# Half-width products of a graph attention issued in a fixed order, with one third of them moved behind the next tile

## The chip, the cores and the metric

The kernel runs on one core of a Trainium2 chip. The metric is the device time of one execution in microseconds (us): 3205.59 is the median of three runs before the change. The core's engines are TensorE (PE; its weight loads are PEld), VectorE (DVE), ScalarE (ACT), GpSimd (POOL) and SyncE (SP); each works through its own instructions in an order fixed when the kernel is built, and waits for the others through semaphores. All data are 32-bit floats.

## The reference, cut to what matters

Two graph layers over 4096 nodes with 512 features in 4 heads of 128. The first layer has an encoder attention, an MLP, a decoder attention and another MLP; the second layer is an attention of another kind. The change is in the decoder attention, which multiplies the encoder's attention matrix once more with new values:

```python
sig = jax.nn.sigmoid(f1[:, :, None] + f2[:, None, :])
...
att = ALPHA * long_att + (1.0 - ALPHA) * local_att
...
Yh = emb.reshape(n, H, D).transpose(1, 0, 2)
Y = jnp.einsum('hij,hjd->hid', att, Yh)
Y = jnp.einsum('hnd,hed->hne', Y, W)
Yc = Y.transpose(1, 0, 2).reshape(n, F)
Yc = jax.nn.elu(Yc)
out = _mlp_block(Yc, dec_mlp_W, dec_mlp_b, dec_mlp_bn_gamma, dec_mlp_bn_beta)
```

The unnormalised weight of node i for node j is exp(sigmoid) where the adjacency is 1, and 0 elsewhere. The kernel gets the sigmoid from a Tanh, and the sums that normalise are kept from the encoder.

## The kernel before

**Blocks and tiles.** The decoder attention is one call of `attention` (L836). It has 8 blocks: 4 heads times 2 halves of the target nodes (2048 columns, `TB`). A block goes through 32 weight tiles, j = 0 to 31, each of 128 source nodes by 2048 targets. Of every five tiles the last (j = 4, 9, 14, 19, 24, 29) is read back from memory, where the encoder had put it (L421, on SyncE's queue); the other 26 are made: Tanh on ScalarE (L568), Exp on ScalarE in place (L569), multiplied by the mask on VectorE in place (L570). The mask `a` comes by SyncE (L212).

**Buffers of tiles.** `weight_tile` takes two of every seven tiles from one pool with two buffers and five from another with five. The Tanh of a later tile can start when a buffer of its pool has been read for the last time.

**Products.** TensorE accumulates a block's output (128 features by 2048 targets) in four banks `po`. Every product of the decoder has a stationary operand of 64 columns and writes the lower (g = 0) or upper (g = 1) 64 partitions of a bank, so it uses one side of the array; two products on different sides can run at once. A single tile takes 8 products: 4 banks times 2 sides.

**Pairs.** To save products, 8 pairs of tiles, (5,6), (8,9), ... (26,27), are handled by sums in the manner of Strassen's scheme: 14 products in place of 16. For a pair with tiles e1 and e2, each with a left and a right half of 1024 columns, VectorE makes t0 = e1 left + e1 right (L331), t1 = t0 + e2 right (L335), t2 = t1 + e2 left (L340), and e1's right half becomes e1 right + e2 right: in block 0 on VectorE (L339), in blocks 1 to 7 by an accumulating DMA on POOL's queue (L337). The tiles t0, t1, t2 have two buffers each. The stationary operands z0 to z3 of the pairs (L816 to L822) lie in the tile `w`, which later holds the next MLP's weights. The products of a pair, in `seven` (L342), go to three sums:

- `po[2]`, `po[3]` with z3 and e2 right (2 products), and `po[0]`, `po[1]` with e2 left and t2 (4);
- `aux[0]`, `aux[1]` with e1 left and t1 (4);
- `aux[2]`, `aux[3]` with t0 and the summed e1 right (4): this is called the third sum below.

So `po` and `aux` take all 8 banks, and the two sets change places from block to block. After the last pair, at j = 31, ScalarE copies `aux` out (L369), POOL's queue swaps its halves (L373), and in the next block at j = 2 VectorE adds it all up (`combined`, L383 to L388). At j = 3 VectorE adds `po` (L806, L809); scaling and ELU follow (L684, L830 to L832).

**What sets the order.** The program is written to a library that places each engine's instructions itself, from its own estimate of when operands will be ready and from the order in which they were made. A dependency given by hand, `tc.issue_after(x)`, keeps instructions of the same engine behind x. In the decoder no such dependency ties the products to each other: `halves` (L326) only makes a product. In blocks 1 to 7 of the trace the products are in the order in which they were made; in block 0 they are not.

**At the end.** `decoder_weights` (L824) loads the next MLP's weights into `w` on SyncE's queue. It is made in the last block at j = 28, and waits for the last product that reads z.

Of the kernel before, what the change touches and what calls it, by code (L numbers as in the profile page):

```python
# [39 lines left out]
N, F, H, D, P = 4096, 512, 4, 128, 128  # L40
# [5 lines left out]
TB = 2048  # L46
NTB = N // TB
# [30 lines left out]
HB = TB // 2  # L78
HD = D // 2
# [10 lines left out]
def kernel(ctx, tc, x, xT, adjT, w0, w0T, v0, wencT, wdecT, vecs, w1, w1T, a1, outT):  # L90
    nc = tc.nc
# [131 lines left out]
    def attention(what, keep, pools, weights, values, row_of, out, finish, ebufs, modes=None, invert=None,  # L223
# [25 lines left out]
        spool, made, masks0 = pools, 0, list(masks0)  # L249
# [73 lines left out]
        pairs = [FIRST + STEP * k for k in range(PAIRS)] if fast is not None else []  # L323
        banks8 = [*(bank() for _ in range(7)), bank1()] if fast is not None else []

        def halves(b, g, weight, x, start, stop):  # L326
            return nc.tensor.matmul(b[g * HD:(g + 1) * HD, :], weight, x, start=start, stop=stop)  # L327

        def sums_first(e):
            t = [spool.tile([P, HB], FP, name=f"t{k}", tag=f"t{k}", bufs=2) for k in range(3)]  # L330
# [11 lines left out]
        def seven(k, v, po, aux, t, e1, e2):  # L342

            one = block(v, pairs[k])
            two = block(v, pairs[k] + 1)
            z = [fast[0][:, i, k, :] for i in range(4)]
            first, stop = k == 0, k == PAIRS - 1

            def into(b, g, weight, x, part, aux_bank):
                return halves(b, g, weight, x[:, part * IB:(part + 1) * IB], first and aux_bank, stop and aux_bank)  # L350

            into(po[2], 0, z[3], e2[:, HB:TB], 0, False)
            into(po[3], 1, z[3], e2[:, HB:TB], 1, False)
            for part in range(2):
                into(aux[part], 0, one[:, 0:HD], e1[:, 0:HB], part, True)
                into(aux[part], 1, z[1], t[1], part, True)
            for part in range(2):
                into(po[part], 0, two[:, 0:HD], e2[:, 0:HB], part, False)
                into(po[part], 1, two[:, HD:D], t[2], part, False)
            for part in range(2):  # L360
                into(aux[2 + part], 0, z[0], t[0], part, True)
                made = into(aux[2 + part], 1, z[2], e1[:, HB:TB], part, True)
            return made

        def aux_out(h, tb, aux, m):
# [27 lines left out]
        for n, (h, tb) in enumerate(blocks):  # L393
# [14 lines left out]
            for j in range(NJ):  # L408

                with pinned(products_of):  # L410
                    for f in later.pop(j, []):
                        f()
                with pinned([a_load, *products_of, last_main] if j else []):
                    if (n, j) in extras:
                        extras[n, j](a_load)
                    if not last and j == NJ - 10:
                        next_row = next_row_of(*blocks[n + 1])
                e = weight_tile()
                store = j % KEEP == KEEP - 1 and kept is not None
                if store and kept == "read":  # L420
                    a_load = nc.sync.dma_start(e, ekeep[h][tb][j // KEEP])  # L421
                else:
                    if masks0:
                        a, a_load = masks0.pop(0)
                    else:
                        a = mask_tile(keep)
                        a_load = load_mask(a, tb, j)

                    with pinned([*(products_of[:1] if kept == "read" and n == 0 and j < 8 else ()),
                                 *(behind if n == 0 and j < EP else ())]):  # L430
                        products_of = weights(e, rowb, a, j, h, SB if NJ * n + j < in_parts0 else 1)


                    if stores and (store if n > 1 else j % KEEP == KEEP - 3):
                        k, t = stores.pop()
                        (nc.sync if n > 1 else nc.scalar).dma_start(ekeep[h][tb][k], t)
                    if store:
                        stores.append((j // KEEP, e))

                if j in pairs:  # L440
                    e1, sums_of = e, sums_first(e)
                elif j - 1 in pairs:
                    made_sums = sums_second(sums_of, e1, e, n > 0)
                    products_of = products_of[0], made_sums

                def products():
                    nonlocal last_main, last_ones
                    if fast is not None:
                        if j - 1 in pairs:
                            last_main = seven(pairs.index(j - 1), values[h], po, aux, sums_of, e1, e)  # L450
                        elif j not in pairs:
                            for s, b in enumerate(po):
                                for g in range(2):
                                    f = (g + s // (SB - 1)) % 2
                                    last_main = halves(b, g, block(values[h], j)[:, f * HD:(f + 1) * HD],
                                                       e[:, s * IB:(s + 1) * IB], j == 0, j == NJ - 1)
                        return

                    with tc.issue_after(last_ones.ins) if last_ones is not None else nullcontext():

                        if j == EVICT:
                            po.append(bank())
                            for k, t in ahead:
                                nc.tensor.matmul(po[-1], block(values[h], k), t[:, (SB - 1) * IB:SB * IB],
                                                 start=(k == 0), stop=False)
                        for s, b in enumerate(po):
                            last_main = nc.tensor.matmul(b, block(values[h], j), e[:, s * IB:(s + 1) * IB],  # L467
                                                         start=(j == 0), stop=(j == NJ - 1))
                    last_ones = None


                if last and invert is not None and j >= NJ - (1 if kept is not None else 4):
                    late.append((j, e))
                else:
                    products()
                if j < EVICT and fast is None:
                    ahead.append((j, e))
                if fast is not None and j == pairs[-1] + 1:
                    m = []
                    at(NJ - 1, aux_out, h, tb, aux, m)  # L480
                    if not last:
                        at(2, combined, h, tb, m)
                if invert is not None:
                    if j in moved:

                        for into_half, e_half in in_parts(2, into, e):
                            nc.gpsimd.dma_start(into_half, e_half, **({"accum_op": ALU.add} if j > moved[0] else {}))  # L487
                    elif j in by_ones:
                        held.append(e)
                    else:  # L490
                        adds.append(e)
                        if last and kept is not None and j >= NJ - 6:
                            at_end.append(e)
                        elif len(adds) == 2:
                            nc.vector.tensor_add(acc, *adds)
                        elif len(adds) > 2:
                            nc.vector.tensor_add(acc, acc, e)  # L497

                    if j == NJ - 1:
                        for t in at_end:  # L500
                            nc.vector.tensor_add(acc, acc, t)

                    if held and j + 1 not in by_ones:
                        with tc.issue_after(last_main.ins):
                            for t in held:
                                add_to_den(den, t, not begun)
                                begun = True
                        held = []
                    if j == NJ - 1:
                        with tc.issue_after(last_ones.ins) if last_ones is not None else nullcontext():  # L510
                            if moved and not ends_later:
                                add_to_den(den, into, not begun)
                                begun = True
                            add_to_den(den, acc, not begun, not ends_later)
# [60 lines left out]
    with tc.tile_pool(name="keep", bufs=1) as keep:  # L575
# [259 lines left out]
        with tc.tile_pool(name="dec", bufs=1) as spool:  # L835
            attention("dec", keep, spool, tanh_weights, xc, lambda h, tb: (rows[tb], h), out_dec, (scaled, elu), 5,  # L836
                      kept="read", behind=behind_it, fast=(z, xd, stationaries),
                      extras={(H * NTB - 1, 28): decoder_weights})


    v1 = xd
# [283 lines left out]
```

## Time and profile before

| what | us |
|---|---|
| median of the runs (3205.39 to 3206.06) | 3205.59 |
| the profiled execution: its own time | 3206.21 |
| the profiled execution: its span on the core | 3204.4 |
| decoder attention, from its first product to its last, at 1182.8 and 2028.6 | 845.8 |
| granted TensorE clock over the execution | 0.996 |

Times in the profile count from the start of the span. A row of a timeline gives the start, the duration, the engine, the line, the operation, output <- inputs, the shape and the number of instructions that were merged; in brackets stands how long the engine had been idle, and what ended that. A product of 32-bit floats leaves two records, each written down as 0.59 us long; records that follow one another on one side of the array start 0.43 us apart, and those of the two sides overlap. The name `ps` stands for seven of the banks, and `den` for the eighth; `e,R` is a weight tile with a value block, `t` a sum, `w` the stationary operands z.

### The profile page before, as it was taken

To read this page: it belongs to the slowest core of one execution; us is meant where nothing else is said; L and a number is where in the kernel's file an instruction comes from. 1 tells how busy PE (TensorE), PEld (TensorE's weight loads), DVE (VectorE), ACT (ScalarE), POOL (GpSimd) and SP (SyncE) were. 2 spreads that over 40 slices of the span, in tenths; PEclk is the share of its full clock that TensorE was granted. 3 is DMA by queue.
4 is the path that set the end of the run, shared out by engine and by line. 5 is a ranking of instruction groups with operands and counts; after the bars stand their busy time and mean duration, and the time that the engine had idled before them with its cause. 6 is when DMAs were issued, how large, how long until landed. Compare 5 with 4: busy or idle time off the path is not lost.

```text
span 3204.4 us, 30115 instructions
## 1 busy us (share of the span) xinstructions
PE 3146.2 (98%) x10467; PEld 1375.5 (43%) x10467; DVE 2944.2 (92%) x2229; ACT 2570.7 (80%) x1825; POOL 567.8 (18%) x740
## 2 busy tenths in 40 slices
PE   7999999999999999999999999999999999999998
PEld 6334444444444464333333333458544444444443
DVE  7989999999999679999999999785699999999998
ACT  7999999999998449999999999456755665666663
POOL 3001211211211000111111111026312222222211
PEclk9999999999999999999999999999999999999999
DMA  9998988988987013667776676331579999999986
GB/s 211 198 193 252 270 223 229 269 221 231 271 230 193 7 43 128 193 188 205 211 200 181 202 217 183 104 112 60 157 188 234 215 221 243 219 214 229 234 213 157
DMA packets 223433, 620.71 MB, mean 194 GB/s; under 512 B 26832, under 2 KB 29936, under 8 KB 207280
## 3 DMA queue, kind: packets, MB, share of 16 engines
q0 software_dynamic: 79648, 263.41, 43.2%
q1 hardware_dynamic: 132200, 332.53, 30.3%
q10 hardware_dynamic: 11432, 22.85, 2.0%
q8 instruction: 82, 1.34, 0.2%
q14 instruction: 71, 0.58, 0.1%
HBM read 378.15 MB, written 84.30 MB: 144 GB/s over the span
## 4 chain that ended last, share of the span: by engine, by line
PE 39%; DVE 29%; issue 14%; DMA 10%; ACT 8%; DVEq 0%; POOL 0%; SPq 0%; ACTq 0%; POOLq 0%
PE ps L467 13%; PE ps L327 9%; DVE e L1042 7%; DVE R L497 7%; PE ps L736 7%; DVE e L570 6%; DMA w<-e 4%; ACT e L568 4%; PE ps L947 3%; ACT e L569 3%; DVE acc L497 3%; DMA a<-mask 2%; DMA e<-e 2%; PE den L327 2%; DMA acc<-e 2%
## 5 line engine op out<-in xcount | busy, mean ns | idle before, releaser
L467 PE MATMUL ps<-e,R 128*128 128x512 f32 x3992 | 1740.4, 596 | 22.3 <-DVE e L570 19.4
L467 PEld LDWEIGHTS ps<-e,R 128*128 128x128 f32 x3992 | 754.9, 191 | 1004.0 <-issue 918.7
L570 DVE TENSOR_TENSOR e<-e,a 128x2048 f32<-128x2048 f32 (+1 forms) x470 | 1048.4, 2256 | 83.0 <-ACT e L569 69.8
L568 ACT ACTIVATE e<-rowb,score 128x2048 f32<-128x2048 f32 (+1 forms) x470 | 909.7, 1970 | 34.4 <-PE ps L327 16.4
L569 ACT ACTIVATE e<-e 128x2048 f32<-128x2048 f32 (+1 forms) x470 | 863.8, 1877 | 2.1 <-ACT e L568 0.2
L327 PE MATMUL ps<-e,R 128*64 128x512 f32 x2304 | 711.2, 593 | 1.6 <-DVE e L570 1.5
L1041 ACT ACTIVATE e<-rowb,nq,jcol 128x2048 f32<-128x2048 f32 x224 | 459.5, 2088 | 266.1 <-DMA w<-e 143.9
L1042 DVE SCALAR_TENSOR_TENSOR e<-e,jcol,a 128x2048 f32<-128x2048 f32 (+1 forms) x265 | 591.3, 2261 | 2.8 <-ACT e L1041 2.8
L327 PEld LDWEIGHTS ps<-e,R 128*64 128x64 f32 x2304 | 224.8, 137 | 264.1 <-issue 261.6
L497 DVE TENSOR_TENSOR R<-R,e 128x2048 f32<-128x2048 f32 x128 | 291.1, 2274 | 0.0
L497 DVE TENSOR_TENSOR acc<-acc,e 128x2048 f32<-128x2048 f32 x121 | 276.3, 2283 | 0.9
L487 POOL DMA_DIRECT2D w<-e x178 | 149.5, 848 | 609.4 <-DMA w<-e 300.4
L736 PE MATMUL ps<-R,w 128*128 128x512 f32 x512 | 220.4, 592 | 0.6 <-DVE w L694 0.6
L487 POOL DMA_DIRECT2D acc<-e x146 | 122.5, 885 | 517.4 <-DMA acc<-e 217.5
L327 PE MATMUL ps<-t,w 128*64 128x512 f32 x448 | 209.5, 594 | 0.1
L327 PE MATMUL ps<-e,w 128*64 128x512 f32 x384 | 183.6, 593 | 3.6 <-DMA e<-e 3.6
L736 PEld LDWEIGHTS ps<-R,w 128*128 128x128 f32 x512 | 97.1, 190 | 123.0 <-issue 117.2
L327 PE MATMUL ps<-t,R 128*64 128x512 f32 x256 | 120.7, 594 | 3.1 <-DVE t L340 3.1
L327 PE MATMUL den<-e,R 128*64 128x512 f32 x256 | 121.2, 592 | 0.0
L947 PE MATMUL ps<-w1x,hT 128*128 128x260 f32 x512 | 115.5, 384 | 1.4 <-ACT hT L925 1.4
L337 POOL DMA_DIRECT2D e<-e x56 | 49.0, 874 | 337.1 <-DVE e L570 184.7
L947 PEld LDWEIGHTS ps<-w1x,hT 128*128 128x128 f32 x512 | 96.5, 190 | 19.9 <-issue 3.3
(210 smaller groups left out, 2219.7 us busy)
## 6 DMA issues: line engine op xcount, KB each, us to landing
a<-mask SPq DMA_DIRECT2D x720, 256.0 KB, 4.4
w<-e POOLq DMA_DIRECT2D x178, 512.0 KB, 6.6
acc<-e POOLq DMA_DIRECT2D x146, 512.0 KB, 7.0
e<-ekeep SPq DMA_DIRECT2D x48, 1024.0 KB, 5.1
ekeep<-e SPq DMA_DIRECT2D x36, 1024.0 KB, 7.0
e<-e POOLq DMA_DIRECT2D x56, 512.0 KB, 5.4
mask<-in_adjT POOLq DMA_DIRECT2D x8, 2048.0 KB, 104.0
rowb<-rows SPq DMA_DIRECT2D x16, 1024.0 KB, 6.8
```

The costliest lines, as they stand in the source:

```text
L327: return nc.tensor.matmul(b[g * HD:(g + 1) * HD, :], weight, x, start=start, stop=stop)
L337: nc.gpsimd.dma_start(e1[:, HB:TB], e2[:, HB:TB], accum_op=ALU.add)
L467: last_main = nc.tensor.matmul(b, block(values[h], j), e[:, s * IB:(s + 1) * IB], start=(j == 0), stop=(j == NJ - 1))
L487: nc.gpsimd.dma_start(into_half, e_half, **({"accum_op": ALU.add} if j > moved[0] else {}))
L497: nc.vector.tensor_add(acc, acc, e)
L568: nc.scalar.activation(e, rowb, AF.Tanh, bias=column(score[:, 1], j, h), scale=0.5)
L569: last_act = nc.scalar.activation(e, e, AF.Exp, scale=0.5)
L570: last_dve = nc.vector.tensor_mul(e, e, a)
L736: last = nc.tensor.matmul(z, w[:, fb, o * P:(o + 1) * P], nodes(src[fb], ib), start=(fb == 0), stop=(fb == C - 1))
L947: m = nc.tensor.matmul(banks[k][:, 0:2 * DX], hT[:, fb, c * P:(c + 1) * P], w1x[:, fb, 2 * k:2 * k + 2, :].rearrange("p h x -> p (h x)"), ...
L1041: last_act = nc.scalar.activation(e, rowb, AF.Relu, bias=column(nq, j, h), scale=column(jcol, j, h))
L1042: last_dve = nc.vector.scalar_tensor_tensor(e, e, column(jcol2, j, h), a, ALU.add, ALU.mult)
```

## The change

The products of the decoder are chained by hand: each is issued behind the one made before it. As they are made with the sides alternating, they alternate everywhere. In `seven`, the third sum's four products are no longer made with the pair: they are put aside in `waiting`, and made right behind the 8 products of the next single tile (j + 2 of the pair's first tile j). Within the pair, what is left keeps its order. The load of the next MLP's weights moves from j = 28 to j = 29 of the last block, since the last pair's third sum, which reads z, now follows tile 28.

```diff
+        last_half, waiting = None, []
+
         def halves(b, g, weight, x, start, stop):
-            return nc.tensor.matmul(b[g * HD:(g + 1) * HD, :], weight, x, start=start, stop=stop)
+            nonlocal last_half
+            with tc.issue_after(last_half.ins) if last_half is not None else nullcontext():
+                last_half = nc.tensor.matmul(b[g * HD:(g + 1) * HD, :], weight, x, start=start, stop=stop)
+            return last_half
...
             for part in range(2):
                 into(po[part], 0, two[:, 0:HD], e2[:, 0:HB], part, False)
-                into(po[part], 1, two[:, HD:D], t[2], part, False)
-            for part in range(2):
-                into(aux[2 + part], 0, z[0], t[0], part, True)
-                made = into(aux[2 + part], 1, z[2], e1[:, HB:TB], part, True)
+                made = into(po[part], 1, two[:, HD:D], t[2], part, False)
+
+            def rest():
+                for part in range(2):
+                    into(aux[2 + part], 0, z[0], t[0], part, True)
+                    into(aux[2 + part], 1, z[2], e1[:, HB:TB], part, True)
+                return last_half
+
+            waiting.append(rest)
             return made
...
                                     last_main = halves(b, g, block(values[h], j)[:, f * HD:(f + 1) * HD],
                                                        e[:, s * IB:(s + 1) * IB], j == 0, j == NJ - 1)
+                            if waiting:
+                                last_main = waiting.pop()()
                         return
...
-                      extras={(H * NTB - 1, 28): decoder_weights})
+                      extras={(H * NTB - 1, 29): decoder_weights})
```

## The prediction

> **What bounds the kernel now.** I read the page first, to place the edited stage, then the time between blocks of that stage, then single rows. All edited lines serve the decoder's attention, whose products are those of L327.
>
> ```profile
> span 3204.4 us, 30115 instructions
> PE 3146.2 (98%) x10467; PEld 1375.5 (43%) x10467; DVE 2944.2 (92%) x2229; ACT 2570.7 (80%) x1825; POOL 567.8 (18%) x740
> ...
> L327 PE MATMUL ps<-e,R 128*64 128x512 f32 x2304 | 711.2, 593 | 1.6 <-DVE e L570 1.5
> ```
>
> TensorE looks full everywhere, but a busy share can't tell a full array from one of which half idles. So I cut the decoder where each block's first product starts, and list for four of the eight blocks the length and the busy time of each engine:
>
> ```profile
> core 0: us, PE busy (x) PEld busy (x) DVE busy (x) ACT busy (x) POOL busy (x), PEclk, DMA share, GB/s
> 1182.79:1296.92 114.13, 112.45 (x481) 44.05 (x481) 98.34 (x61) 107.14 (x61) 3.23 (x6) 1.00 0.45 148
> 1296.92:1402.74 105.82, 103.92 (x483) 36.99 (x481) 100.74 (x75) 102.02 (x62) 16.19 (x21) 1.00 0.70 196
> ...
> 1506.62:1610.11 103.49, 103.22 (x482) 34.23 (x480) 100.00 (x74) 101.06 (x61) 16.16 (x21) 1.00 0.70 201
> 1610.11:1715.55 105.44, 103.67 (x483) 34.17 (x481) 98.72 (x73) 101.63 (x61) 12.42 (x18) 1.00 0.70 197
> ```
>
> A product is two records, a block is 240 products. Where they alternate, TensorE's timeline shows 78 records from 1610.12 to the next row at 1626.86, so 16.74/39 = 0.429 us a product. A block thus can't be shorter than 240 x 0.429 = 103.0 us. The eight together take 845.8 against 824.1: **21.7 us is all that any order of products can win**, 11.1 of it in block 0 and 10.6 in blocks 1 to 7. ScalarE (101 to 102) and VectorE (99 to 101) are close behind. Where the excess lies:
>
> ```profile
> 1610.12 17.32 PE L327 MATMUL ps<-e,R 128*64 128x512 f32 x78
> ...
> 1224.35 1.88 PE L327 MATMUL ps<-e,R 128*64 128x512 f32 x4
> 1226.07 1.35 PE L327 MATMUL ps<-t,w 128*64 128x512 f32 x3
> ...
> 1349.90 0.64 PE L327 MATMUL ps<-e,w 128*64 128x512 f32 x1 [1.43 <-DMA e<-e]
> ...
> 1630.93 0.64 PE L327 MATMUL ps<-t,R 128*64 128x512 f32 x1 [0.48 <-DVE t L340]
> ```
>
> In block 0 four records take 1.72 us from 1224.35 to 1226.07: one at a time, both products on one side. Counting each step between starts beyond 0.429: block 0 has 2.4 us of waits, so 8.7 went to sides that did not alternate. Blocks 1 to 7 already run in the order made; they lose 4.8 to the accumulating DMA (1.64 of it at 1349.90, others in blocks 4, 5 and 7) and 4.6 to the sum t2 of the first pair, 0.66 in each block.
>
> **What the skill says.** "TensorE: Matmul & The Clock Gate", Part 3, has products on distinct column groups run at once, starts about 4 ns apart, and matmuls strictly in issue order. The trace agrees: partners start 6 ns apart or less (1630.93 and 1630.94), and the order counts. I go by the trace's 0.429. The same page's table of specifications calls ScalarE's and VectorE's queues strictly first in, first out; the trace can't contradict it, and rows below show ScalarE idle behind one wait. That is what the rival on the other side rests on.
>
> **The change, part by part.** Instructions stay the same in number and shape; products, sums, activations and DMAs all do. Only order and waits move.
>
> (1) Strict order, block 0. Its ceiling is 8.7, but the operands come from VectorE, which runs from 1200.44 to 1278 with pauses under 0.5 us. I lay products of 0.429 in the new order against VectorE's own ends. Pair (5,6) must wait for e2 until 1202.8 and for t2 until 1206.3, and ends at 1207.6; tile 7 is made at 1208.5, so TensorE idles 0.9 where the old order had the third sum to do. Pair (11,12) waits for t1 until 1226.7 and t2 until 1229.0, and ends at 1230.2; with the third sum, still owed, that is where the old order stood at 1232.0. So **up to 1232 the alternation returns nothing**. From there the singles 13 to 31 and the pairs from 14 follow with waits at 17 (1.3 us) and 23 (1.3 us) for t1 and t2, and the last single ends at 1295.4, against 1296.9: 1.5 us gained, if VectorE keeps its order. Bounds: VectorE's last sum (t2 of pair 26) ends at 1278.3, and 39 products follow its first user's turn, 16.7 us, so 1295.0 in that order; if VectorE put tiles 27 and 28 elsewhere, up to 8.7 could come back; if its sums come later, 2 us are lost.
>
> (2) Third sum later. Its last factor, e1 after the accumulating DMA, is wanted 8 products x 0.429 = 3.43 us later. The longest wait for it is 1.64, so **the 4.8 us go**. They don't merely move to t2: ScalarE's last tiles of a block wait for buffers that TensorE frees, so TensorE earlier means t2 earlier too. The t2 waits themselves stay, except that block 1 starts with ScalarE ahead (its 2.43 and 3.54 us below shrink): 0.7 more.
>
> (3) Buffers freed later. Counted from a pair's first product, TensorE frees now e2 at 3.9, e1 at 6.0, the next single at 9.4. After: e2 at 3.9, single at 7.7, e1 at 9.4. The third is no later, the second is by 1.72, or by 3.43 where the single's buffer belongs to the other pool (2 of 7 tiles do). ScalarE feels exactly this release:
>
> ```profile
> 1256.44 2.01 ACT L568 ACTIVATE e<-rowb,score 128x2048 f32<-128x2048 f32 x1 [2.43 <-PE ps L327]
> ...
> 1272.98 3.90 ACT L568 ACTIVATE e<-rowb,score 128x2048 f32<-128x2048 f32 x2 [3.54 <-PE den L327]
> ...
> 1537.80 2.00 ACT L568 ACTIVATE e<-rowb,score 128x2048 f32<-128x2048 f32 x1 [1.28 <-PE ps L327]
> 1540.36 2.01 ACT L568 ACTIVATE e<-rowb,score 128x2048 f32<-128x2048 f32 x1 [0.56 <-PE ps L327]
> ...
> 1585.45 4.13 ACT L568 ACTIVATE e<-rowb,score 128x2048 f32<-128x2048 f32 x2
> ```
>
> And it counts, as the chain of waits through the end of block 3 shows (start, us, what):
>
> ```profile
> 1582.38 5.17 PE ps L327 x24
> 1587.57 2.01 ACT e L568
> 1589.58 3.59 ACT e L569 x2
> ...
> 1616.46 4.50 DVE e L570 x3
> ...
> 1630.93 2.36 PE ps L327 x9
> ```
>
> TensorE frees a buffer, ScalarE fills it at 1587.57 and runs on to the block's first tiles, VectorE masks and sums them, t2 is ready at 1630.9, TensorE waited. Every link is tight, so a delay of ScalarE there comes back whole. Queued behind the waiting Tanh are Exps; if one is put ahead of it (1.80 us: two in 3.59 at 1589.58), 1.72 is covered and costs nothing, and 3.43 leaves 1.6. If not, 1.72 or 3.43 a block. Nothing below zero: no release is earlier but the single's. I take 0.3 a block, 2.1 in all, since the two Tanhs and two Exps can swap freely; both ends go into the range.
>
> (4) t0 is also read 3.43 later and has two buffers. In block 1, t0 of pair 14 is written at 1332.57, while pair 8's reads would end at 1330.3 + 3.4 = 1333.8: VectorE would wait 1.2. Pair 14's t2 ends at 1342.5 and is wanted at 1343.2 + 7 x 0.429 = 1346.2: free, by 2.5 us.
>
> (5) The end. The third sum of the last pair ends 10.3 us before the stage instead of 13.7. Behind it: two ScalarE copies, the swaps on POOL's queue, VectorE's combination, all 3.4 later at most; head 3 is complete at 2037.2 and not wanted before 2028.7 + 21 x 0.858 = 2046.7. The next weights, whose DMA sits in SyncE's queue for TensorE's last read of z, start at 2015.06 and DMA traffic is over by about 2022.3; 3.4 later is 2025.7, against 2028.7. SyncE has nothing of the decoder behind it. POOL's accumulations keep place and triggers. Without this cover each could cost up to 3.4 once.
>
> **Sum**, against the profiled execution's own time, 3206.2 (span 3204.4 and 1.8 around it; the median is 3205.6, 0.6 lower): -1.5 - 4.8 - 0.7 + 2.1 = -4.9. On the median: **3200.7**.
>
> **Rivals.**
> - *Block 0 recovers all.* VectorE's order adapts to the new order of products: -8.7 - 4.8 = -13.5, 3192. For it: ScalarE waits 6 us for TensorE in block 0, so TensorE lags there. Against: VectorE has no pause before 1278.
> - *ScalarE waits in order* (the other side). At the second freed buffer it waits 1.72 in four blocks and 3.43 in three: +17.2 - 7.0 = +10.2, 3216. Against: Exps can fill. For: at 1537.80 and 1540.36 the trace has just such a pair of Tanhs in order, with 0.56 idle between, though an Exp was to be done. It decides once ScalarE loses over 1.0 us a block (7.0/7).
> - *Nothing is left.* The first half of the change alters only block 0, since blocks 1 to 7 are in that order already; if block 0 stays bound by VectorE and the DMA waits go into ScalarE's, 3205 within 2.
>
> **How the numbers follow.** Likeliest 0.40 (3197 to 3205), all-recovered 0.15, ScalarE in order 0.33 (3208 to 3223), nothing left 0.12. No change means within 0.2%, 6.4 us. Faster: a third of the first (0.13) and the second, 0.28. Slower: three quarters of the third, 0.24. Same: 0.48. Range 3192 to 3216: half of the second case and 0.13 of the third fall outside.
>
> **What would show it.** Block 0 at 112.6 us, with no records one at a time, and new waits for t1 and t2; no wait on the accumulating DMA in TensorE's rows; t2 waits near 0.7 in each block. If they grow to 2 us or more, with ScalarE's idle on TensorE above 24 us in all, the third case holds. A difference outside 1182 to 2029 us would have none of my reasons.

## The result and the profile after

| | before | after |
|---|---|---|
| median, us (lowest to highest) | 3205.82 (3205.39 to 3206.44) | 3226.05 (3223.75 to 3229.34) |
| ratio | | 1.0064 [1.0046, 1.0081] |
| profiled execution: its own time, span | 3206.21, 3204.4 | 3225.43, 3223.6 |
| decoder, first product to last | 845.3 | 866.7 |
| from the start of the span to the decoder | 1182.8 | 1182.6 |
| after the decoder | 1176.3 | 1174.4 |

The median before is of four runs here, the three of the table above and one more. The decoder is counted in this document from the start of its first product to the start of its last (1182.8 to 2028.1 before), so it reads 0.5 us shorter than in the table above.

The change made the kernel slower by 0.64%. I had forecast 3200.7 with a range of 3192 to 3216: the sign was wrong, and the time lies outside. The whole loss, 21.3 us, lies in the decoder; what stands before it and behind it didn't lose.

The page of the kernel after. In it L327 of before is L331; Tanh, Exp and mask are L580, L581 and L582; t0, t1 and t2 are L336, L340 and L345.

```profile
span 3223.6 us, 30102 instructions
PE 3148.9 (98%) x10467; PEld 1366.8 (42%) x10467; DVE 2947.2 (91%) x2229; ACT 2575.1 (80%) x1825; POOL 568.3 (18%) x740
...
L331 PE MATMUL ps<-e,R 128*64 128x512 f32 x2304 | 704.7, 594 | 1.9 <-DVE e L582 1.8
...
L331 PE MATMUL ps<-t,R 128*64 128x512 f32 x256 | 122.1, 599 | 14.0 <-DVE t L345 13.7
```

The work is the same: PE busy is 2.7 us more of 3149, and the instruction counts in this row are equal. New is the idle time ahead of the products that read t2, 14.0 us.

The decoder cut by blocks, five of eight (from and to in us, the length, then the busy time of each engine, the granted clock):

```profile
core 0: us, PE busy (x) PEld busy (x) DVE busy (x) ACT busy (x) POOL busy (x), PEclk, DMA share, GB/s
1182.56:1297.07 114.51, 107.60 (x482) 34.66 (x483) 101.72 (x65) 110.32 (x63) 3.23 (x6) 1.00 0.45 148
1297.07:1400.92 103.85, 103.85 (x483) 34.77 (x480) 97.35 (x70) 99.31 (x59) 16.42 (x21) 1.00 0.70 195
...
1508.75:1619.39 110.64, 105.80 (x482) 35.28 (x480) 102.51 (x75) 102.23 (x61) 16.68 (x21) 0.98 0.68 187
1619.39:1727.41 108.02, 105.48 (x483) 35.14 (x480) 99.97 (x76) 102.50 (x61) 12.42 (x18) 1.00 0.70 195
1937.29:2049.20 111.91, 104.59 (x481) 35.12 (x478) 97.04 (x75) 87.55 (x53) 12.34 (x18) 1.00 0.62 162
```

Block 1 does what was hoped: 103.85, without a wait. Blocks 3 and 7 (the third row and the last) are 7 us longer than before. Block 0 is no shorter than before, 114.51 against 114.13, although its products now alternate: PE is busy for 107.6 instead of 112.5, and the gain went into waits.

What TensorE waits for in the decoder, over all:

```profile
engine line waited for: us in total, times, longest us
PE ps L331 <- DVE t L345: 13.7, 13, 2.9
PE ps L331 <- DVE t L340: 8.3, 7, 1.9
PE ps L331 <- DVE e L582: 3.6, 5, 1.5
```

The accumulating DMA is gone from this list (3.6 before). Instead t2 stands at 13.7 (3.1 before) and t1 at 8.3. Counted from start to start, beyond 0.429 us a product, t2 grew from 4.2 to 16.8, t1 from 0.4 to 9.7, and the DMA fell from 4.5 to nothing.

Who is late? The chain of waits through the wait of block 3 that is longest (start, us, what):

```profile
1556.83 8.21 DMA e<-e
...
1565.12 2.01 ACT e L580
1567.14 0.02 issue
1567.16 1.92 ACT e L581
1569.08 0.02 issue
1569.10 0.04 DVE e L582
1569.14 2.17 issue
1571.31 1.23 DVE t L345
1572.54 0.04 issue
1572.58 5.77 PE ps L331 x17
```

Read backwards: TensorE starts at 1572.58, as soon as t2 is made. VectorE's mask ran from 1569.10 to 1571.3 (the row "issue" of 2.17), behind an Exp, behind a Tanh. The Tanh at 1565.12 waited for its buffer, 2.60 us, and what freed it was the accumulating DMA, which had read it. So the tile is late, and its sum with it, because ScalarE got a buffer late.

ScalarE in blocks 1 to 7 (1297 to 2060 us; the groups with their idle time ahead, and who ended it):

```profile
L580 ACT ACTIVATE e<-rowb,score 128x2048 f32<-128x2048 f32 x177 | 348.8, 1994 | 32.2 <-PE den L331 14.6 <-PE ps L331 10.5 <-DMA e<-e 7.0
...
L842 ACT ACTIVATE exd<-R 128x512 f32<-128x512 f32 x32 | 19.8, 619 | 21.9 <-DVE R L696 17.6 <-DVE R L844 4.3
L379 ACT COPY R<-ps 128x512 f32<-128x512 f32 x25 | 13.6, 577 | 7.1 <-PE ps L331 7.1
```

The same rows of before had 19.2 (Tanh; 18.1 of it by TensorE, 0.7 by the DMA), 17.9 (ELU's Exp) and 2.3 us (the copy of `aux`). Together 39.4 became 61.2, which is 21.8 more; blocks 1 to 7 together became 21.0 longer. That the two are so close is in part chance, for not all of this idle time is in the way. ScalarE's last Exp of the decoder ends at 2031.0, and behind it there is no tile left to make; there fall 6.7 of the copy's 7.1 us, most of them in one wait:

```profile
2038.70 0.58 ACT L379 COPY R<-ps 128x512 f32<-128x512 f32 x1 [5.42 <-PE ps L331]
```

There fall also 17.2 of the 21.9 us ahead of ELU, and before the change all of the copy's and ELU's waits lay there. What is left is 13.0 us more ahead of the Tanh (7.0 more on buffers that TensorE frees, 6.3 more on buffers that the DMA frees, a little less on the rest), and 4.7 ahead of ELU, whose Exps the library has put at other places. **So most of the loss, 17.7 us of 21.0, goes with ScalarE standing idle between its tiles**, and the larger part of that is waiting for buffers.

### The profile page after: what moved, and what is told of

It reads as the page before. It is cut to its first block, busy times and chain, and to the rows that moved or that the text cites. A ratio compares the mean times of both kernels' runs of the same rounds, so it can differ in the third digit from the quotient of the medians.

```text
span 3223.6 us, 30102 instructions
## 1 busy us (share of the span) xinstructions
PE 3148.9 (98%) x10467; PEld 1366.8 (42%) x10467; DVE 2947.2 (91%) x2229; ACT 2575.1 (80%) x1825; POOL 568.3 (18%) x740
## 4 chain that ended last, share of the span: by engine, by line
PE 22%; DVE 18%; issue 10%; ACT 5%; DMA 2%; DVEq 0%; POOL 0%; ACTq 0%; POOLq 0%
PE ps L479 10%; DVE R L509 5%; DVE e L1054 5%; PE ps L748 3%; DVE e L582 3%; PE ps L331 3%; PE ps L959 3%; ACT e L580 3%; ACT e L581 2%; DVE t L340 1%; DMA a<-mask 1%; DMA e<-e 1%; PE den L331 1%; DVE t L336 0%; ACT e L1053 0%
## 5 line engine op out<-in xcount | busy, mean ns | idle before, releaser
L582 DVE TENSOR_TENSOR e<-e,a 128x2048 f32<-128x2048 f32 (+1 forms) x470 | 1050.4, 2260 | 94.9 <-ACT e L581 81.4
L580 ACT ACTIVATE e<-rowb,score 128x2048 f32<-128x2048 f32 (+1 forms) x470 | 909.9, 1973 | 43.1 <-PE den L331 14.6
L581 ACT ACTIVATE e<-e 128x2048 f32<-128x2048 f32 (+1 forms) x470 | 866.4, 1882 | 4.1 <-DVE e L582 1.1
L331 PE MATMUL ps<-e,R 128*64 128x512 f32 x2304 | 704.7, 594 | 1.9 <-DVE e L582 1.8
L331 PEld LDWEIGHTS ps<-e,R 128*64 128x64 f32 x2304 | 221.4, 137 | 270.6 <-issue 266.1
L331 PE MATMUL ps<-t,w 128*64 128x512 f32 x448 | 213.8, 594 | 8.4 <-DVE t L340 8.3
L331 PE MATMUL ps<-e,w 128*64 128x512 f32 x384 | 149.1, 594 | 2.0 <-DVE e L582 1.8
L331 PE MATMUL ps<-t,R 128*64 128x512 f32 x256 | 122.1, 599 | 14.0 <-DVE t L345 13.7
L331 PE MATMUL den<-e,R 128*64 128x512 f32 x256 | 119.9, 592 | 0.0
```

The costliest lines, as they stand in the source:

```text
L331: last_half = nc.tensor.matmul(b[g * HD:(g + 1) * HD, :], weight, x, start=start, stop=stop)
L580: nc.scalar.activation(e, rowb, AF.Tanh, bias=column(score[:, 1], j, h), scale=0.5)
L581: last_act = nc.scalar.activation(e, e, AF.Exp, scale=0.5)
L582: last_dve = nc.vector.tensor_mul(e, e, a)
```

## The experiments

In each run the ratio is to the kernel before on the same chip. "Above before" is the difference of the medians. The theories at the start: (a) the tile e1 and the sum t0 are held 3.43 us longer, and ScalarE has no slack for it; (b) the library, which estimates times itself, sorts ScalarE's and VectorE's work differently for the new order of products, and badly.

| run | what | median | above before | ratio | decoder |
|---|---|---|---|---|---|
| e1_chain | strict order alone | 3204.30 | -2.6 | 0.9992 [0.9983, 1.0001] | 843.5 |
| e2_late | late third sum alone | 3231.61 | +24.8 | 1.0078 [1.0062, 1.0093] | 870.7 |
| e3_half | third sum 1.72 us late | 3210.19 | +3.3 | 1.0009 [1.0002, 1.0016] | 849.3 |
| e4_fourbufs | before, 4 buffers for 5 | 3247.17 | +40.3 | 1.0127 [1.0112, 1.0142] | 885.4 |
| e5_late_pin | after, masks behind t2 | 3236.85 | +29.7 | 1.0093 [1.0078, 1.0108] | 874.8 |
| e6_chain_pin | e1_chain, masks behind t2 | 3212.99 | +5.9 | 1.0018 [1.0011, 1.0024] | 852.8 |
| e7_half_pin | e3_half, masks behind t2 | 3217.59 | +10.5 | 1.0035 [1.0023, 1.0047] | 856.5 |
| e8_quarter | third sum 0.86 us late | 3215.57 | +8.4 | 1.0028 [1.0016, 1.0039] | 853.6 |
| e9_late_order1 | after, e1_chain's order elsewhere | 3238.77 | +29.4 | 1.0095 [1.0078, 1.0112] | 879.4 |
| e10_chain_order2 | e1_chain, after's order elsewhere | 3241.15 | +31.8 | 1.0102 [1.0087, 1.0117] | 881.4 |
| e11_half_order1 | e3_half, e1_chain's order elsewhere | 3221.50 | +12.2 | 1.0040 [1.0025, 1.0055] | 859.9 |
| e12_hold_e1 | e1 held 3.43 us longer, no more | 3267.01 | +60.2 | 1.0182 [1.0166, 1.0197] | 898.2 |
| e13_hold_none | its control | 3205.58 | -1.3 | 0.9995 [0.9986, 1.0003] | 842.0 |
| e14_hold_t0 | t0 held instead | 3219.24 | +12.4 | 1.0037 [1.0023, 1.0051] | 855.3 |
| e17_late_one | after, t1 and t2 in one buffer | 3229.62 | +23.1 | 1.0073 [1.0058, 1.0088] | 869.3 |
| e15_late_six | the same, 6 tile buffers | 3210.83 | +4.3 | 1.0013 [1.0006, 1.0020] | 849.3 |
| e16_chain_six | e1_chain, same buffers as e15 | 3199.10 | -7.4 | 0.9979 [0.9970, 0.9987] | 838.7 |

### Which half of the change costs

e1_chain is the kernel before with the chain alone; the third sum stays with its pair, and the load of weights at j = 28:

```diff
+        last_half, waiting = None, []
...
-            return nc.tensor.matmul(b[g * HD:(g + 1) * HD, :], weight, x, start=start, stop=stop)
+            nonlocal last_half
+            with tc.issue_after(last_half.ins) if last_half is not None else nullcontext():
+                last_half = nc.tensor.matmul(b[g * HD:(g + 1) * HD, :], weight, x, start=start, stop=stop)
+            return last_half
```

> Only the strict order; the third sum stays with its pair. Late buffers (the third sum keeps e1's buffer 3.4 us longer, ScalarE and then the sums come late): near the kernel before, 3202 to 3208, with its waits on the accumulating DMA (4.8 us) and one t2 wait of 0.7 in each of blocks 1 to 7. Strict order itself costs (products that could have filled a wait for t1 or t2 are held back): 3218 to 3226, with t1 and t2 waits as in the changed kernel.

e2_late is the kernel after without the chain:

```diff
-            with tc.issue_after(last_half.ins) if last_half is not None else nullcontext():
-                last_half = nc.tensor.matmul(b[g * HD:(g + 1) * HD, :], weight, x, start=start, stop=stop)
+            last_half = nc.tensor.matmul(b[g * HD:(g + 1) * HD, :], weight, x, start=start, stop=stop)
```

> Only the later third sum, without the chain. Late buffers: 3218 to 3228, the decoder within 4 us of the changed kernel's 866.7 us. Strict order: 3200 to 3208.

The strict order alone gains 1.45 us in block 0 (112.68) and nothing that can be told from zero over all. The late third sum alone costs 24.8. Its time lies above the 3218 to 3228 that I expected, its decoder 4.0 us from the changed kernel's, as expected. So the loss is that part's, and in e1_chain the waits on the DMA remain, as they did before:

```profile
PE ps L331 <- DVE t L345: 4.1, 10, 0.5
PE ps L331 <- DMA e<-e: 3.8, 5, 1.4
PE ps L331 <- DVE e L575: 2.8, 3, 1.5
```

### Less delay, fewer buffers

e3_half makes the third sum after 4 of the next single tile's 8 products, e8_quarter after 2:

```diff
-                            if waiting:
-                                last_main = waiting.pop()()
+                                if waiting and s == 1:
+                                    last_main = waiting.pop()()
```

> As the changed kernel, but the third sum stands behind 4 of the next single tile's 8 products, so that it comes 1.7 us later than in the kernel before and not 3.4. Late buffers: a part of the loss, 3208 to 3218. Strict order: as the changed kernel, 3222 to 3228.

> The third sum behind 2 of the next tile's 8 products, 0.86 us later than in the kernel before. Late buffers: between strict order alone (3204) and half (3210), so 3204 to 3208, with most of the 4.6 us of waits on the accumulating DMA gone and about as much back at t2. Placement: no order by size, anything from 3198 to 3215.

e4_fourbufs is the kernel before with one tile buffer less:

```diff
-            attention("dec", keep, spool, tanh_weights, xc, lambda h, tb: (rows[tb], h), out_dec, (scaled, elu), 5,
+            attention("dec", keep, spool, tanh_weights, xc, lambda h, tb: (rows[tb], h), out_dec, (scaled, elu), 4,
```

> The kernel before with 4 tile buffers in the larger pool in place of 5, nothing else. Late buffers: one buffer less costs like a buffer held for a whole tile, 3.2 us, but at every tile: slower by 15 us or more, with new t1 and t2 waits inside the blocks and ScalarE idle on TensorE. If buffers are not the limit: within 6 us of the kernel before.

Taking away a buffer costs 40 us: the kernel before has no buffer to spare, which speaks for (a). The waits are only in part of after's kind: TensorE's steps ahead of t2's products lose 16.3 us, but 11.1 more go to the accumulating DMA, and ScalarE's Tanh waits 26.0 us for that DMA and 13.6 for TensorE. The delays don't give a monotone row either: 0.86 us late costs 8.4, 1.72 late costs 3.3, and 3215.57 lies outside both ranges given for e8_quarter. In it ELU's Exps on ScalarE wait for VectorE, some 2 us in a block; the library has moved them. That alone doesn't make a kernel slow: in e16_chain_six below, the fastest of all, they wait longer. As long as the library sorts each kernel anew, a delay can't be priced.

### Is it the place of the masks?

In after, VectorE does the mask of the tile behind a pair ahead of the pair's t2 in some places. e5_late_pin forbids that, and e6 and e7 do the same to e1_chain and e3_half:

```diff
+        made_sums = None
...
-                        products_of = weights(e, rowb, a, j, h, SB if NJ * n + j < in_parts0 else 1)
+                        with tc.issue_after(made_sums.ins) if made_sums is not None else nullcontext():
+                            products_of = weights(e, rowb, a, j, h, SB if NJ * n + j < in_parts0 else 1)
```

> The changed kernel with one more order by hand: VectorE may not mask the tile after a pair before it has made that pair's t2. Placement (t2 waits because the builder put it behind a masking that itself waits for ScalarE): most of the 16.8 us of t2 waits go, 3208 to 3216. Late buffers alone (ScalarE's tiles come late whatever VectorE does first): 3220 to 3230, the waits turning from t2 to t1 or to tiles.

> Strict order without the later third sum, with the same order by hand on VectorE. Placement: the t2 wait at the head of each block, 0.63 each, shrinks as well, 3198 to 3203. Late buffers: no change against the strict order alone, 3202 to 3207.

> The third sum behind 4 of the next tile's 8 products, with the order by hand on VectorE. Placement: its 13.4 us of t2 waits go, 3197 to 3203, below the kernel before. Late buffers: 3207 to 3212, as without it.

All three lost, and all three lie above the ranges of both theories. In e5_late_pin TensorE's steps lose 0.4 us for t2, but 29.6 for tiles:

```profile
PE ps L331 <- DVE e L584: 24.1, 23, 3.8
PE ps L331 <- DMA e<-e: 2.4, 3, 1.9
PE ps L331 <- DVE t L340: 0.5, 1, 0.5
```

So t2 behind a mask isn't what costs: with t2 first, the tile comes late. VectorE itself waits 45.6 us for ScalarE's Exps there (52.6 in after), which fits tiles that come late from ScalarE. The order by hand has a price of its own, though: it costs e1_chain 8.5 us and e3_half 7.1.

### The same order on all other engines

Here every instruction of the decoder on ScalarE, VectorE and POOL is tied, by dependencies without a semaphore, to the one that stood ahead of it in another kernel's order. Only TensorE's order then differs (SyncE's isn't held).

```diff
+            made = nc.done()
+            for engine, order in ORDERS.items():
+                for i, k in zip(order, order[1:]):
+                    tc.add_manual_dep(made[engine][k], made[engine][i].name,
+                                      mybir.DependencyInfo(mybir.DependencyClass.NoSync, mybir.DependencyReason.DATA),
+                                      reason="order")
```

> The changed kernel's TensorE order, late third sum included, with ScalarE's, VectorE's and POOL's instructions of the decoder held in the order that they have in the run with the strict order alone (e1_chain). Late buffers: 3218 to 3230, the old order of the other engines doesn't help, and ScalarE waits for TensorE. The builder's re-sorting of the other engines: 3200 to 3208.

> The reverse: the third sum stays with its pair (TensorE's order of e1_chain), and ScalarE, VectorE and POOL are held in the order of the changed kernel. Late buffers: 3202 to 3210. Re-sorting: 3215 to 3226.

> The third sum behind 4 of the next tile's 8 products (1.7 us later), the other engines in the order of e1_chain. Late buffers: 3205 to 3211, as with its own order (3210). Re-sorting: 3199 to 3204, since the waits on the accumulating DMA go and nothing else changes.

Above before, in us:

| TensorE's order | others in e1_chain's order | others in after's order |
|---|---|---|
| third sum with its pair | -2.6 (e1_chain) | +31.8 (e10) |
| 1.72 us late | +12.2 (e11) | |
| 3.43 us late | +29.4 (e9) | +20.2 (after) |

All three lie above what theory (a) gave for them, by 9 to 31 us: it had the sign of e9 right, and none of the sizes. e10 lies above the range of (b) as well, but on its side, and shows that an order made for the late third sum costs 34.4 us where the third sum is early. Each order of the other engines fits its own order of products. With the order held, a delay of 1.72 costs 14.8 and one of 3.43 costs 32.0, about in proportion. So (b) is rejected as the source of the loss: the loss is there without the library's new order, which gave 9 of 32 us back. Whether some third order would give back more isn't shown. In e9 ScalarE's waits in blocks 1 to 7 are these (a helper makes all its instructions, so all have its line, L163, and go by their tiles):

```profile
ACT e L163 <- PE ps L432: 25.3, 14, 3.7
ACT e L163 <- PE den L432: 24.9, 11, 3.7
```

Its tiles wait 50.2 us for TensorE against 17.6 in e1_chain: 32.6 more, about the 32.0 lost.

### One hold at a time

What is held longer, e1's buffer or t0's? e12 to e14 are e1_chain with its order held as above, and one product more for each pair: two columns of zeros, added to a sum that is open anyway, right behind the next single tile's 8 products. Its stationary operand is what is to be held. Nothing else moves.

```diff
+            waiting.append(e1[:, HB:HB + HD])
...
+                            if waiting:
+                                with tc.issue_after(last_half.ins):
+                                    last_half = nc.tensor.matmul(po[2][0:HD, 0:2], waiting.pop(), zero,
+                                                                 start=False, stop=False)
```

In e13_hold_none the operand is a constant, in e14_hold_t0 it is t0.

> The order of e1_chain on all four engines, the third sum with its pair, plus one tiny product per pair behind the next single tile, which takes 64 columns of e1's right half as stationary operand and multiplies them by zeros: e1's buffer is held 3.4 us longer and nothing else moves. e1's buffer: slower than e13_hold_none by 20 to 35 us. Another cause: within 5 us of it.

> The price of the tiny product: the same, reading a constant instead of e1. Both theories: 64 of them at up to 0.4 us, 3205 to 3230 (no claim on which).

> The same, reading t0. e1's buffer the cause: within 3 us of e13_hold_none. t0's two buffers: slower than it by 10 us or more.

The product itself costs nothing that can be told from noise (3205.6). Reading e1 with it costs **61.4 us**, on average 0.96 for each of 64 holds, and twice what was expected; reading t0 costs 13.7, which is what was expected if t0's hold counts too. ScalarE in e12, blocks 1 to 7 (L568 is the small product; this was the fastest of e12's four executions, 8 us below the median):

```profile
ACT e L163 <- PE ps L434: 24.5, 11, 3.8
ACT e L163 <- PE den L434: 23.4, 9, 3.7
ACT e L163 <- PE ps L568: 21.6, 10, 4.8
```

69.5 us in all, and for 21.6 of it the small product itself is what a Tanh waits for, up to 4.8 us at once. VectorE in e14:

```profile
DVE t L163 <- PE den L434: 9.9, 7, 3.6
DVE t L163 <- PE ps L434: 7.0, 6, 1.9
```

VectorE stands 16.9 us ahead of a t0, and what comes late behind it is the accumulating DMA: TensorE's steps lose 9.5 us to it, against 1.1 in e13. In after VectorE has no such wait ahead of t0, and TensorE none for the DMA. So t0's hold has a price where the rest runs on time; that it cost anything in after isn't shown.

e12 costs more than e9, in which e1 is held just as long. Two things differ: in e9 the single tile's products come 1.72 us earlier, and its buffer too, and in e12 the third sum still needs the DMA early (17.8 us of TensorE's steps against 1.2 in e9). How much each of the two makes up was not taken apart.

### One buffer more

If holds are what costs, another buffer should make up for one. There is no room for it unless t1 and t2 get one buffer each in place of two; e17_late_one is after with that alone, e15_late_six has the sixth buffer too, and e16_chain_six makes both edits to e1_chain.

```diff
-            t = [spool.tile([P, HB], FP, name=f"t{k}", tag=f"t{k}", bufs=2) for k in range(3)]
+            t = [spool.tile([P, HB], FP, name=f"t{k}", tag=f"t{k}", bufs=1 if k else 2) for k in range(3)]
...
-            m.extend(spool.tile([P, HB], FP, name=f"t{k}", tag=f"t{k}", bufs=2) for k in range(2))
+            m.extend(spool.tile([P, HB], FP, name=f"t{k}", tag=f"t{k}", bufs=1 if k else 2) for k in range(2))
...
-            attention("dec", keep, spool, tanh_weights, xc, lambda h, tb: (rows[tb], h), out_dec, (scaled, elu), 5,
+            attention("dec", keep, spool, tanh_weights, xc, lambda h, tb: (rows[tb], h), out_dec, (scaled, elu), 6,
```

> The changed kernel with one buffer each for t1 and t2 in place of two, as a control: it makes room for a sixth tile buffer. If the next pair's sums have to wait for TensorE's last read, VectorE shows waits for TensorE ahead of t1 or t2, and the time is above the changed kernel's 3226 by up to 10 us; if the sums are read before the next pair's are due, it stays within 4 us of it. Both theories allow either.

> The same with a sixth buffer in the larger pool of tiles. If the hold of e1's buffer is the cause, one more buffer makes up for it: at least 15 us below the run with one buffer for t1 and t2 and five tiles, ScalarE's idle ahead of its Tanh from 32 us to under 15 in blocks 1 to 7, t2 waits of TensorE under 6. If the library's placement of the other engines is the cause, it stays within 5 us of that run and the t2 waits above 12.

> Strict order alone, the third sum with its pair, with one buffer each for t1 and t2 and six tile buffers. The decoder's blocks 1 to 7 are 5.4 us a block or less above the floor of 103.0 already (7.2 us of 728 over all seven in the strict order with five), so under both theories it gains at most 8 us on 3204; under the buffer theory the third sum's delay costs it little, so that it and the late third sum with six buffers lie within 6 us of one another; under the placement theory they lie over 15 apart.

The sixth buffer gives back 18.8 us, e15 against e17. The late third sum costs 22.8 with five buffers (after against e1_chain) and 11.7 with six: half of it. The idle time ahead of the Tanh falls from 38.2 us in e17 to 19.5, by 18.7, which fits the time won; but it isn't under 15, and TensorE's steps still lose 14.3 to t2, not under 6. So the expectation held for the time and not for the rows. The two kernels with six buffers lie neither within 6 us of one another nor over 15 apart. The sixth buffer also changes which tiles go to which pool, and the library sorts anew, so 18.8 is the price of the buffer with all that follows from it.

Much of the other 11.7 us has a path of its own in e15's trace, which neither theory named. Here are POOL's first step in making z for the next head, its issue of the second swap, and VectorE's `combined` behind that, at the head of block 2:

```profile
1389.94 3.33 POOL L831 TENSOR_TENSOR w<-R 128x512 f32<-128x512 f32 x1 [2.79 <-PE ps L331]
...
1399.34 1.06 POOL L383 DMA_DIRECT2D t<-R  x2
...
1403.57 0.69 DVE L395 TENSOR_TENSOR t<-t,t 64x512 f32<-64x512 f32 x1 [2.38 <-DMA t<-R]
```

The third sum is the last to read z and the last to write `aux`. POOL waits for it, the swap is issued behind that (in e16 already at 1390.49), and VectorE waits 2.38 us for the swap. From there to the block's last t2, at 1490.4, VectorE pauses 0.3 us in all, so it never catches up: TensorE waits 1.57 and 0.52 us for t2 in the first two pairs and 1.29 in the last. VectorE waits for a swap like this, 2.4 to 3.5 us, at the head of each of blocks 2 to 7 in e15, 16.4 us in all, and never there in e16. Blocks 2, 4 and 6, where a new head begins, are 9.1 us longer than e16's, of 10.7 for the whole decoder. How much of it the delay itself brings, and how much the place that the library gave to the copies and to POOL's work, no run takes apart.

e16_chain_six beats both kernels: 0.9979 [0.9970, 0.9987]. Five of its eight blocks:

```profile
1181.96:1295.55 113.59, 106.97 (x481) 34.34 (x482) 101.78 (x67) 111.33 (x64) 3.23 (x6) 0.98 0.46 149
1295.55:1398.55 103.00, 103.00 (x482) 34.48 (x480) 98.15 (x71) 99.70 (x60) 16.50 (x21) 1.00 0.73 204
1398.55:1501.55 103.00, 103.00 (x482) 34.48 (x480) 97.62 (x72) 100.60 (x60) 12.39 (x18) 1.00 0.71 200
1501.55:1604.80 103.25, 103.22 (x482) 34.39 (x480) 99.59 (x74) 100.75 (x61) 16.47 (x21) 1.00 0.71 201
...
1916.75:2021.20 104.45, 104.03 (x483) 34.33 (x479) 97.53 (x78) 86.91 (x53) 13.01 (x19) 1.00 0.62 172
```

Blocks 1 and 2 stand at 103.00, which is 240 products of 0.429: TensorE never waits. (Before the run I had put what stands above the floor in e1_chain's blocks 1 to 7 at 7.2 us; it is 9.7, 730.8 against 721.1.) And ScalarE's Tanh hardly waits, in blocks 1 to 7:

```profile
ACT e L573 <- PE den L331: 1.3, 2, 0.8
ACT e L573 <- PE ps L331: 1.1, 3, 0.6
```

The accumulating DMA, for whose sake the third sum was moved, costs TensorE 0.2 us here. That reads as if the missing buffer had made the DMA late as well, since it can't start before its two tiles are there; no run shows this by itself, and the kernel before wasn't tried with six buffers.

## Why the prediction was wrong

By its own steps:

1. **Strict order, block 0.** -1.5, to 112.6 us: measured alone, 112.68. Right, and with new waits for t1 and t2 as laid out. In the whole change the late third sum takes it back, to 114.51, with a wait of 1.46 us for t1 at 1278.01 that the prediction didn't have.
2. **The waits on the DMA go.** Right for TensorE (4.5 us to nothing). That they "don't merely move to t2" was wrong in part: ScalarE now waits 7.0 us for buffers that the same DMA frees, and t2 comes late behind that, as the chain through 1565.12 shows.
3. **Buffers freed later: the step that failed.** It put 0.3 us a block for it, "since the two Tanhs and two Exps can swap freely". Blocks 1 to 7 became 21.0 us longer although they won 4.5 from the DMA waits, so the price was 25.5 us in seven blocks, 3.6 a block, twelve times the term. Free swaps were the wrong assumption: with the order held, the delay costs 32 us, and all the re-sorting that the library does gives back 9. I counted one release per block, the one at a block's end where the chain was seen to be tight. A block has eight pairs, and they count together: the 64 holds cost 32.0 us in e9, 0.5 each on average, and 61.4 in e12, 0.96 each.
4. **t0's second buffer, "free, by 2.5 us".** In after VectorE doesn't wait ahead of t0, so the time wasn't lost there. But the margin doesn't exist as a rule: held alone, t0 costs 13.7 us.
5. **The end of the stage.** Free, as said; what follows the decoder is 1.9 us shorter, and the copies of `aux` wait longer only in the last block, behind the last tile. But the step looked at this end alone. The copy, the swap and z come round at the other blocks too: in the changed kernel VectorE waits just 1.0 us for a swap there (at 1404.51), in e15 16.4.

The rival "ScalarE waits in order" had the mechanism and the sign, and named the sign that would show it (t2 waits above 2 us, ScalarE's idle on TensorE above 24: 16.8 in eight blocks and 25.1). Its 17.2 us were still too few, as it also counted only the release at one pair of each block. Giving it 0.33 beside 0.40 for a gain, with a term of 0.3 that rested on no row, was the error of judgement: the row at 1537.80 and 1540.36, two Tanhs in order with an Exp left undone, was evidence against free swaps, and I had named it as such.

One reading of the prediction is off, without a sum that rests on it: partners start 7 ns apart in the row that it cites, and some 60 ns apart in others (1325.56 and 1325.62), not 6 or less.

## What to carry to other kernels

Ahead of moving a reader later, list what it is the last to read, and count every hold, not only the one at the place where the chain is seen to be tight. Where ScalarE and VectorE were both some 95% busy, a hold of 3.43 us cost on average 0.5 us (e9) to 1 us (e12). A tiny extra reader, here too cheap to measure, tells in one run which buffer counts, though not the price of the change itself (61.4 us against 32.0). And ahead of reordering around a late operand, try a buffer more: in e16_chain_six the waits on the DMA were down to 0.2 us without the late third sum.

## What the runs showed of the hardware

An idle stretch of TensorE can cost more than itself. After the wait of 2.60 us that ended at 1572.58 (by the ends that the profile models), four products took 0.85 us each in place of 0.43, from 1573.49 to 1576.87; after one of 2.94 us that ended at 2001.76 none did. In e17_late_one two waits of the same length, 2.99 us, ended at 1577.31 and 2006.25, and slow products followed the first alone, so the length of the wait doesn't settle it. Stretches of the timeline ahead of, in and behind the slow part, and then around the second wait (the granted clock is the third number from the end):

```profile
1569.00:1572.50 3.50, 0.99 (x6) 0.11 (x2) 3.40 (x3) 3.50 (x3) 0.00 (x0) 1.00 0.15 48
1572.50:1577.30 4.80, 4.72 (x14) 1.46 (x16) 4.80 (x6) 4.80 (x4) 0.85 (x1) 0.64 0.54 128
1577.30:1582.00 4.70, 4.70 (x24) 1.58 (x22) 4.70 (x4) 3.37 (x3) 0.00 (x0) 1.00 0.45 92
...
2001.70:2006.00 4.30, 4.24 (x20) 1.49 (x22) 4.30 (x6) 3.93 (x3) 0.86 (x1) 1.00 0.69 207
```

The clock was 0.64 over the middle stretch and full on both sides, so the slow part lasted 3.4 us and took 1.6 us more. The Trainium skill ("TensorE: Matmul & The Clock Gate", Part 1) has a free-running window of about 3.4 us after which the clock is halved or restored; the length of the slow part agrees with that, while its condition of a whole idle window isn't what this trace has, as 2.6 us of idle were enough. The other thing not expected was how little a product of two columns costs: 64 of them could not be told from noise (e13_hold_none is 1.3 us below the kernel before on its chip, e1_chain 2.6 below it on another, and both intervals reach 1.000).
